# First image and its conv kernels ahead of the constants, constants on ScalarE's queue, attention weights in few transfers

## The chip, the cores and the metric

The kernel runs on one core of one Trainium2 chip. The metric is the device time of one launch in microseconds (us). The engines are TensorE (PE, with its weight loads PEld), VectorE (DVE), ScalarE (ACT), GpSimd (POOL) and SyncE (SP), which computes nothing and issues transfers (DMAs). Each engine takes its instructions in the order of its own queue; an instruction that waits holds everything behind it on that queue.

## The reference

There are 32 images of 128 channels by 64 x 64 pixels, in float32.

```
x = x + conv(group_norm(x))      # per-image 3x3 kernel: sum of 4 kernels with softmax(sigmoid(fc(mean))) weights
t = tokens(x)                    # 4096 tokens of 128 features an image
t = t + LN(z + gate * up(windowed_attention(down(z))))      # z = LN(t); window 144, stride 72, 4 heads of 4
t = t + scan(batch_norm(W LN(t)))                           # y = sigmoid(wx_t + V y), over the tokens of a row
```

The batch norm needs the statistics of all images, so the scan can't begin before the last image has gone through everything else.

## The kernel before, in words

**Constants and guards.** At the top, `ident` and masks made from it are computed, and 14 small tensors are fetched on SP's queue (`nc.sync.dma_start`; `column`, line 297, does the one-column ones). From some of these the kernel computes two flags on VectorE, ScalarE and TensorE (lines 353 to 403): `oki`, whether the attention scores are bounded so that no maximum has to be subtracted, and `okv`, whether the scan contracts so that it can be cut in runs. Each engine loads `oki` into a register and branches on it (line 1843) to `images`; `okv` is loaded before the second branch (line 1999), to `by_runs`.

**Images.** `images` (line 413) holds the first phase. Two frames of 66 x 66 pixels (`frames`, `xs`) take the images in turn. `fetch(b)` brings an image in 4 transfers of 16 rows; images 0 and 1 are fetched at the head of `images`, a later one at the head of its `load` (line 597). For each image there are 13 generators:

- `load`: group-norm statistics (`mv`, `gm`, `cv`), the routing weights `pl` and `co`, and the mixed conv kernel `h`, summed from four kernels of 576 KB, which `kernel()` (line 629) fetches into buffers called `place`. Two are asked for ahead of the statistics' second half and each further one when a buffer has been used.
- `taps` and `waves`: transformed kernels `w` and transformed inputs `u` of a short convolution that yields four output rows from six products. `conv`: the products on TensorE into the PSUM banks `nm`. `drain`: the results added into the frame.
- `project`: frame to DRAM (`x_d`), layer norm over channels, down-projection. `feed`, `values`, `attend`: queries and keys, values, and scores (`sc`), exponentials on ScalarE (`ex`, `ext`) and weighted sums (`av`). `divide0` and `divide1`: division and up-projection (`avs`).
- `tail` and `last`: the two layer norms behind the attention, the product with W (`fWc`), the results to DRAM (`z_d`, `out`).

**Setup.** `setup` (line 1267) is a job of its own. It builds what the attention needs: block-diagonal copies of the query, key and value weights (`wqB`, `wkB`, `wvB`: zero fill on GpSimd and 8 transfers of a 16 x 16 block each), repeated biases (`bqB`, `bkB`, `bd`: 8 transfers each), masks, the folded output weights `wc` (four products `wuT,aw` of TensorE, each followed by three steps of VectorE), and constants of `VT` (56 copies). `project` waits for it.

**The order of the work.** All jobs are Python generators that yield before each step what it needs: engine, PSUM pool, operands read and written. A planner at build time (lines 1385 to 1417) keeps a model of when each engine is free (class `Clock`) and always takes the step that it expects to be ready first; between equal ones it takes the smaller of "image number + due time", with the due times from the table `DUE` (line 41). So the queues are written out in full when the program is built, and a due time that is changed can move instructions anywhere. A job that isn't in the table, as `setup` isn't, comes ahead of all others that are ready at the same time. In the traces all planned instructions stand on line 241, the planner's wrapper.

**Second phase.** `by_runs` (line 1871) cuts the tokens in runs of 32 with 20 warming steps, and steps through them on TensorE, VectorE, ScalarE and GpSimd.

Of the kernel before, what the change touches and what calls it, by code (L numbers as in the profile page):

```python
# [20 lines left out]
NH = 4  # L21
HD = 4
DK = NH * HD
WIN = 144
HALF = WIN // 2
NWG = 7
# [4 lines left out]
NR = 20  # L31
NQ = 8
# [4 lines left out]
NI = 2  # L37
NSTR = 4


DUE = {
    "load": (-0.91, 0.63, 29),
    "taps": (-0.09, 0.03, 6),
    "waves": (-0.12, 0.52, 26),
    "conv": (-0.43, 1.01, 36),
    "drain": (-9.0, 0.0, 14),
    "project": (0.75, 0.5, 33),
    "feed": (1.63, 0.54, 27),
    "values": (1.27, 1.15, 28),
    "attend": (1.24, 1.1, 89),  # L50
    "divide0": (1.92, 0.12, 15),
    "divide1": (2.3, 0.02, 11),
    "tail": (2.55, 0.45, 33),
    "last": (3.05, 0.62, 40),
}

# [200 lines left out]
def hybrid_kernel(  # L257
# [24 lines left out]
    nc = tc.nc  # L282
# [7 lines left out]
    const = ctx.enter_context(tc.tile_pool(name="const", bufs=1))  # L290
# [5 lines left out]

    def column(src, name):
        t = const.tile([P, 1], F32, name=name)
        nc.sync.dma_start(t, src.rearrange("(c o) -> c o", o=1))
        return t  # L300


    ident = const.tile([P, P], F32, name="ident")
    make_identity(nc, ident)
# [15 lines left out]


    fcwT = const.tile([P, NK], F32, name="fcwT")
    nc.sync.dma_start(fcwT, fc_wT)
    fcb = const.tile([P, NK], F32, name="fcb")
    nc.sync.dma_start(fcb, fc_b.partition_broadcast(P))
    wd = const.tile([P, 32], F32, name="wd")
    nc.vector.memset(wd, 0.0)
    nc.sync.dma_start(wd[:, 0:DK], w_downT)
    gsig = const.tile([P, 1], F32, name="gsig")
    nc.sync.dma_start(gsig, gate.partition_broadcast(P))  # L330
# [8 lines left out]
    nc.sync.dma_start(fWT, ffn_WT)  # L339
    fVT = const.tile([P, P], F32, name="fVT")  # L340
    nc.sync.dma_start(fVT, ffn_VT)
    fg = column(ffn_gamma, "fg")
    fb = column(ffn_beta, "fb")

    bdr = const.tile([P, DK], F32, name="bdr")
    nc.sync.dma_start(bdr, b_down.partition_broadcast(P))
    ipr = const.tile([P, 3 * DK], F32, name="ipr")
    nc.sync.dma_start(ipr, in_proj_b.partition_broadcast(P))
    ipT = const.tile([DK, 3 * DK], F32, name="ipT")
    nc.sync.dma_start(ipT, in_projT)  # L350
# [36 lines left out]
    with tc.tile_pool(name="sb2", bufs=1) as sb2, tc.tile_pool(  # L387
        name="ps2", bufs=1, space=bass.MemoryType.PSUM
# [16 lines left out]
    small = nc.values_load(oki[0:1, 0:1], min_val=0, max_val=1)  # L405


    frames = const.tile([P, NI, (H + 2) * (W + 2)], F32, name="frames")
    framed = frames[:, :, 0:T]

    QT, NPL, NF, NZ, NU = T // 4, 5, 2, 3, 9

    def images(nc):
# [6 lines left out]
        with ExitStack() as pa:  # L420
# [3 lines left out]
            def rows(t, i, n=8):  # L424
                return t[:, 1 + i : 1 + i + n, 1 : W + 1]

            def fetch(b):
                for i in range(4):
                    nc.sync.dma_start(rows(xs[b % NF], 16 * i, 16), x[b, :, 16 * i : 16 * i + 16, :])

            fetch(0)


            for b in range(1, NF):
                fetch(b)
            keep = pa.enter_context(tc.tile_pool(name="keep", bufs=1))
            big = pa.enter_context(tc.tile_pool(name="big", bufs=NZ))
            one = pa.enter_context(tc.tile_pool(name="one", bufs=1))
# [7 lines left out]
            nc = clock  # L446
# [140 lines left out]
            def load(b):  # L587
# [5 lines left out]
                ):  # L593
                    yield
                gx = xs[b % NF]
                if b >= NF:
                    fetch(b)
                yield "DVE", None, (rows(gx, 0, H),)
                st = sml.tile([P, NBLK, 6], F32, name="st")
                for i in range(NBLK):  # L600
# [26 lines left out]
                taps = []  # L627

                def kernel():
                    w = yield from place("SP", ())  # L630
                    nc.sync.dma_start(w, conv_k[:, len(taps)].rearrange("m i j l -> m (i j l)"))
                    taps.append(w)

                for k in range(2):
                    yield from kernel()
                yield "PE", nms, (cv,)
                gv_ps = clock.take("PE", nms)
# [629 lines left out]
            def setup():  # L1267

                nonlocal wqB, wkB, wvB, bqB, bkB, bd, wd2, mqk, mvt, VEs, Vc, VTf, VT, wc, fWc, gbc, gbk, avg
                yield "SP", None, ()  # L1270

                wqkv = []
# [7 lines left out]
                bqB, bkB = kept([P, 1], "bqB"), kept([P, 1], "bkB")  # L1280
                bd = kept([P, 1], "bd", 0.0)
# [6 lines left out]
                in_b1 = in_proj_b.rearrange("(c o) -> c o", o=1)  # L1288
                for g in range(NQ):
                    r = slice(16 * g, 16 * g + 16)  # L1290
                    nc.sync.dma_start(bqB[r], in_b1[0:DK])
                    nc.sync.dma_start(bkB[r], in_b1[DK : 2 * DK])
                for g in range(NQ):
                    nc.sync.dma_start(
                        bd[16 * g : 16 * g + DK], b_down.rearrange("(c o) -> c o", o=1)
                    )

                mqk = kept([P, 2 * NH], "mqk")
                nc.vector.tensor_reduce(
                    mqk, memb.rearrange("p (q g) -> p g q", q=4), axis=AX.X, op=ALU.add  # L1300
                )

                m16 = kept([P, 8], "m16")
                nc.vector.tensor_reduce(
                    m16, ident.rearrange("p (g k) -> p g k", k=16), axis=AX.X, op=ALU.add
                )
# [11 lines left out]
                Vc = kept([P, NWG * NQ * DK], "Vc")  # L1318
                VTf = kept([P, NWG * NQ * NR + 32 - NR], "VT", 0.0)
                VT = VTf[:, 0 : NWG * NQ * NR].rearrange("p (w o) -> p w o", o=NR)  # L1320
                for q in range(4):
                    for u in range(2):
                        for m in range(NWG):
                            nc.vector.tensor_copy(
                                VT[:, NQ * m + 2 * q + u, DK:NR], mvt[:, NH * u : NH * (u + 1), 0]
                            )

# [19 lines left out]
                for q in range(4):  # L1347
                    r = slice(32 * q, 32 * q + DK)
# [36 lines left out]
            done, gone = {}, {}  # L1385
            pa.enter_context(tc.manual_schedule())
            jobs = [["setup", 0, setup(), None, 0]]
            for b in range(NB):
                for name, g in (
                    ("last", last(b)), ("tail", tail(b)), ("divide0", divide(b, 0)), ("divide1", divide(b, 1)), ("attend", attend(b)),  # L1390
                    ("project", project(b)), ("load", load(b)), ("conv", conv(b)), ("feed", feed(b)),
                    ("taps", taps(b)), ("waves", waves(b)), ("values", values(b)), ("drain", drain(b)),
                ):
                    jobs.append([name, b, g, None, 0])
            while jobs:
                near = min(j[1] for j in jobs) + 4
                best = None
                for job in jobs:
# [444 lines left out]
    with tc.If(small > 0) as arm:  # L1843
        images(nc)
# [212 lines left out]
```

## Time and profile before

| | us |
|---|---|
| median of 3 runs | 4645.3 |
| lowest and highest | 4629.8, 4645.8 |
| the profiled execution | 4639.8 |
| its span, first to last instruction | 4637.9 |
| TensorE busy | 4195.7 |
| VectorE busy | 3576.6 |
| ScalarE busy | 2503.6 |
| GpSimd busy | 1649.0 |
| first conv product of TensorE | 78.9 |
| last store of the first phase issued | 4040.2 |

The profile is of one execution. Its page gives the busy time of each engine, and the span in 40 slices of 116 us, with a digit for the tenths that are busy. The trace behind it can be asked for the busy time in any stretch, for the instructions in order of time (start, duration, engine, line, operation, output and inputs, and in brackets the idle time before it with what ended that), and for who waited for whom (total, times, longest). "SPq" is SP's issuing of a transfer, not the transfer itself. A time in a line that joins several instructions reaches from the first to the last.

### The profile page before, as it was taken

The page shows a single profiled execution, that of the slowest core. Times are in us where ns is not written, and L with a number is a line of the kernel's source. Part 1 is how long each engine was busy: PE and PEld are TensorE (multiplying, and loading weights), DVE is VectorE, ACT ScalarE, POOL GpSimd, SP SyncE. Part 2 cuts the span into 40 slices and gives each one's busy share as a digit, 9 for nine tenths or more (in the row PEclk, how much of TensorE's full clock was granted, in tenths as well). Part 3 has the DMA queues.
Part 4 walks back from the last instruction along what each step waited for, and adds up shares of the span by engine and source line. Part 5 has one row for each costly group of instructions (what it writes and reads, how often), then busy time and mean ns, then how long its engine had stood idle before and what let it go on. Part 6 is the DMA issues. An engine that isn't in the chain of part 4 may idle for free.

```text
span 4637.9 us, 102446 instructions
## 1 busy us (share of the span) xinstructions
PE 4195.7 (90%) x41527; PEld 2063.1 (44%) x41527; DVE 3576.6 (77%) x5472; ACT 2503.6 (54%) x4012; POOL 1649.0 (36%) x1656
## 2 busy tenths in 40 slices
PE   3999989999999999999999999999999997389995
PEld 1444444444444444444444444444444443145552
DVE  5877778888878877878887877878788854469994
ACT  0455555555555555545555455555555565258883
POOL 2433333333333333333333333333333321037674
PEclk9999999999999999999999999999999998679997
DMA  3434464554555555555555455555555453439997
GB/s 79 134 120 145 149 198 164 172 175 149 177 167 178 180 161 172 171 163 176 170 177 182 145 190 154 166 173 179 176 159 174 160 182 134 168 151 248 281 263 145
DMA packets 468568, 789.39 MB, mean 170 GB/s; under 512 B 339040, under 2 KB 349296, under 8 KB 435312
## 3 DMA queue, kind: packets, MB, share of 16 engines
q1 hardware_dynamic: 459376, 715.56, 47.3%
q0 software_dynamic: 8704, 67.11, 7.1%
q8 instruction: 332, 5.44, 0.5%
q14 instruction: 156, 1.28, 0.1%
HBM read 499.06 MB, written 276.76 MB: 167 GB/s over the span
## 4 chain that ended last, share of the span: by engine, by line
PE 26%; DVE 15%; DMA 7%; issue 3%; ACT 2%; SPq 2%; POOL 1%; DVEq 0%; ACTq 0%; POOLq 0%
PE nm L241 13%; PE sc L241 6%; PE av L241 4%; DVE v L1921 4%; DVE zt L241 3%; DVE v L1915 2%; SPq L241 2%; DMA place<-r_d 2%; PE v L1920 1%; DMA zr<-z_d 1%; DVE frames L241 1%; DMA place<-x_d 1%; DVE u L241 1%; ACT yw L1924 1%; DMA out_dram<-zr 1%
## 5 line engine op out<-in xcount | busy, mean ns | idle before, releaser
L241 ACT ACTIVATE ex<-sc 128x1152 f32<-128x1152 f32 x896 | 1013.6, 1131 | 879.9 <-PE sc L241 859.3
L241 POOL TENSOR_TENSOR qe<-qs,mqk 128x576 f32<-128x576 f32 x448 | 601.1, 1344 | 864.8 <-PE sc L241 856.3
L241 PE MATMUL nm<-u,w 128*128 128x512 f32 x1536 | 809.1, 631 | 18.9 <-POOL w L241 18.9
L241 PE MATMUL sc<-qe,ks 32*128 32x288 f32 x7168 | 698.0, 459 | 80.4 <-ACT ext L241 33.3
L241 PE MATMUL av<-ex,VE 128*32 128x144 f32 x14336 | 631.0, 294 | 29.7 <-DVE avs L241 29.1
L241 PEld LDWEIGHTS sc<-qe,ks 32*128 32x128 f32 x7168 | 284.9, 185 | 621.5 <-issue 168.0
L241 PEld LDWEIGHTS av<-ex,VE 128*32 128x32 f32 x14336 | 368.1, 110 | 369.1 <-issue 260.8
L241 POOL TENSOR_TENSOR u<-frames 128x528 f32<-128x528 f32 x256 | 374.4, 1475 | 154.8 <-PE nm L241 152.3
L241 PE MATMUL nm<-u,h 128*128 128x512 f32 x768 | 393.0, 620 | 0.0
L241 PEld LDWEIGHTS nm<-u,w 128*128 128x128 f32 x1536 | 253.2, 191 | 276.0 <-issue 245.1
L1920 PE MATMUL v<-yw,fVT 128*128 128x256 f32 x1024 | 327.6, 442 | 40.3 <-ACT yw L1924 39.1
L241 ACT ACTIVATE place<-zt 128x1024 f32<-128x1024 f32 x256 | 264.1, 1054 | 142.4 <-DVE zt L241 121.2
L241 DVE SCALAR_TENSOR_TENSOR u<-u,u 128x528 f32<-128x528 f32 x256 | 263.1, 1044 | 66.8 <-POOL u L241 65.2
L1925 POOL COPY zr<-yw 128x256 f32<-128x256 f32 x416 | 258.7, 689 | 123.4 <-ACT yw L1924 122.7
L1924 ACT ACTIVATE yw<-v,shf 128x256 f32<-128x256 f32 x512 | 242.3, 474 | 106.0 <-DVE v L1921 68.3
L241 PE MATMUL nm<-zt,fWc 128*128 128x512 f32 x512 | 286.5, 651 | 7.8 <-ACT zt L241 6.8
L1921 DVE SCALAR_TENSOR_TENSOR v<-zr,scl,v 128x256 f32<-128x256 f32 x416 | 257.3, 665 | 40.7 <-PE v L1920 40.0
L241 POOL TENSOR_TENSOR kt<-ks,mqk 128x384 f32<-128x384 f32 (+1 forms) x96 | 86.3, 899 | 492.5 <-ACT ks L241 439.4
L241 PE MATMUL nm<-place,avg 128*32 128x256 f32 x3072 | 246.8, 401 | 8.2 <-ACT place L241 7.9
L1914 PE MATMUL v<-yw,fVT 128*128 128x254 f32 x608 | 212.1, 449 | 46.1 <-ACT yw L1911 28.2
L241 DVE SCALAR_TENSOR_TENSOR zt<-sc,gbk,zt 128x576 f32<-128x576 f32 (+1 forms) x192 | 174.9, 911 | 98.0 <-PE sc L241 95.6
L1920 PEld LDWEIGHTS v<-yw,fVT 128*128 128x128 f32 x1024 | 159.8, 194 | 194.6 <-ACT yw L1924 188.3
(205 smaller groups left out, 6676.8 us busy)
## 6 DMA issues: line engine op xcount, KB each, us to landing
place<-r_d SPq DMA_DIRECT2D x384, 512.0 KB
place<-in_conv_k_dram SPq DMA_DIRECT2D x128, 576.0 KB
x_d<-frames SPq DMA_DIRECT2D x32, 2112.0 KB
place<-x_d SPq DMA_DIRECT2D x128, 528.0 KB
frames<-in_x_dram SPq DMA_DIRECT2D x128, 512.0 KB
out_dram<-zt SPq DMA_DIRECT2D x64, 1024.0 KB
z_d<-zt SPq DMA_DIRECT2D x64, 1024.0 KB
zr<-z_d SPq DMA_DIRECT2D x26, 2048.0 KB
```

Of the source, the lines that this page charges most:

```text
L241: got = f(*args, **kw)
L1914: nc.tensor.matmul(ps, fVT, yw[1 - r % 2][:, :, 1:], start=True, stop=True)
L1915: nc.vector.scalar_tensor_tensor(ps, z, scl, ps, ALU.mult, ALU.add)
L1920: nc.tensor.matmul(ps, fVT, yw[1 - r % 2], start=True, stop=True)
L1921: nc.vector.scalar_tensor_tensor(ps, zt[:, :, :, r], scl, ps, ALU.mult, ALU.add)
L1924: nc.scalar.activation(yw[r % 2], ps, AF.Sigmoid, bias=shf)
L1925: nc.gpsimd.tensor_copy(zt[:, :, :, r], yw[r % 2])
```

## The change

Five things are altered; the arithmetic of the images stays.

1. The frames are allocated at the top, and image 0 is fetched there on SP's queue before anything else. Image 1 is fetched at the head of its `load`, as later images are.
2. The 14 constants are fetched by ScalarE's queue.
3. Image 0 asks for its four conv kernels at once at the head of `load`. A fetch of a later image is a step of its own that the planner places.
4. `setup` fetches the in-projection weights with one transfer that repeats them over 8 groups of partitions (`rep`), and each repeated bias with one; the block-diagonal weights are products of `rep` with a mask on VectorE. The 56 copies into `VT` become two. `setup` gets an entry in `DUE`, and waits until image 0's taps are done before it makes the weights.
5. Due times of `taps`, `project`, `divide1` and `tail` are changed.

```diff
 DUE = {
+    "setup": (0.2, 0.2, 8),
-    "taps": (-0.09, 0.03, 6),
+    "taps": (0.2, 0.11, 6),
...
-    "project": (0.75, 0.5, 33),
+    "project": (0.55, 0.51, 33),
...
-    "divide1": (2.3, 0.02, 11),
-    "tail": (2.55, 0.45, 33),
+    "divide1": (2.21, 0.02, 11),
+    "tail": (2.4, 0.8, 33),
...
     def column(src, name):
         t = const.tile([P, 1], F32, name=name)
-        nc.sync.dma_start(t, src.rearrange("(c o) -> c o", o=1))
+        nc.scalar.dma_start(t, src.rearrange("(c o) -> c o", o=1))
...
+    frames = const.tile([P, NI, (H + 2) * (W + 2)], F32, name="frames")
+    framed = frames[:, :, 0:T]
+    for i in range(4):
+        nc.sync.dma_start(
+            frames[:, 0].rearrange("p (h w) -> p h w", w=W + 2)[:, 1 + 16 * i : 17 + 16 * i, 1 : W + 1],
+            x[0, :, 16 * i : 16 * i + 16, :],
+        )
...
-    nc.sync.dma_start(fcwT, fc_wT)
+    nc.scalar.dma_start(fcwT, fc_wT)
...
-            fetch(0)
-            for b in range(1, NF):
-                fetch(b)
...
                 gx = xs[b % NF]
-                if b >= NF:
+                if b:
+                    yield "SP", None, (), (rows(gx, 0, H),)
                     fetch(b)
+                taps = []
+                def kernel():
...
+                if b == 0:
+                    for k in range(NK):
+                        yield from kernel()
...
-                for k in range(2):
+                for k in range(2 if b else 0):
                     yield from kernel()
...
-                    if k + 2 < NK:
+                    if len(taps) < NK:
                         yield from kernel()
...
+                def eight(t, a):
+                    n, w = int(a.shape[0]), int(a.shape[1])
+                    nc.sync.dma_start(
+                        t, a.rearrange("(g d) w -> g d w", g=1).to_broadcast([NQ, n, w])
+                    )
...
+                rep = kept([P, 3 * DK], "rep")
+                eight(rep, in_projT)
+                bqB, bkB, bd = kept([P, 1], "bqB"), kept([P, 1], "bkB"), kept([P, 1], "bd")
+                in_b1 = in_proj_b.rearrange("(c o) -> c o", o=1)
+                eight(bqB, in_b1[0:DK])
+                eight(bkB, in_b1[DK : 2 * DK])
+                eight(bd, b_down.rearrange("(c o) -> c o", o=1))
+                while ("taps", 0, 1) not in done:
+                    yield
+                yield "DVE", None, (rep,)
                 wqkv = []
                 for i, n in enumerate(("wqB", "wkB", "wvB")):
-                    t = kept([P, P], n, 0.0)
-                    for g in range(NQ):
-                        r = slice(16 * g, 16 * g + 16)
-                        nc.sync.dma_start(t[r, r], in_projT[:, i * DK : (i + 1) * DK])
+                    t = kept([P, P], n)
+                    nc.vector.tensor_mul(
+                        t.rearrange("p (g k) -> p g k", k=DK),
+                        rep[:, i * DK : (i + 1) * DK].rearrange("p (g k) -> p g k", g=1).to_broadcast([P, NQ, DK]),
+                        m16.rearrange("p (g k) -> p g k", k=1).to_broadcast([P, NQ, DK]),
+                    )
                     wqkv.append(t)
...
-                for q in range(4):
-                    for u in range(2):
-                        for m in range(NWG):
-                            nc.vector.tensor_copy(
-                                VT[:, NQ * m + 2 * q + u, DK:NR], mvt[:, NH * u : NH * (u + 1), 0]
-                            )
+                yield "DVE", None, ()
+                for u in range(2):
+                    nc.vector.tensor_copy(
+                        VT.rearrange("p (w u) o -> p w u o", u=2)[:, :, u, DK:NR],
+                        mvt[:, NH * u : NH * (u + 1), 0].rearrange("p (w h) -> p w h", w=1).to_broadcast([P, NWG * 4, NH]),
+                    )
```

The other constants change their queue as `fcwT` does.

More of the change, by code (lines that the diff above doesn't have):

```diff
@@ L322, in hybrid_kernel @@
     fcwT = const.tile([P, NK], F32, name="fcwT")
-    nc.sync.dma_start(fcwT, fc_wT)
+    nc.scalar.dma_start(fcwT, fc_wT)
     fcb = const.tile([P, NK], F32, name="fcb")
-    nc.sync.dma_start(fcb, fc_b.partition_broadcast(P))
+    nc.scalar.dma_start(fcb, fc_b.partition_broadcast(P))
     wd = const.tile([P, 32], F32, name="wd")
     nc.vector.memset(wd, 0.0)
-    nc.sync.dma_start(wd[:, 0:DK], w_downT)
+    nc.scalar.dma_start(wd[:, 0:DK], w_downT)
     gsig = const.tile([P, 1], F32, name="gsig")
-    nc.sync.dma_start(gsig, gate.partition_broadcast(P))
+    nc.scalar.dma_start(gsig, gate.partition_broadcast(P))
     nc.scalar.activation(gsig, gsig, AF.Sigmoid)
@@ L338, in hybrid_kernel @@
     fWT = const.tile([P, P], F32, name="fWT")
-    nc.sync.dma_start(fWT, ffn_WT)
+    nc.scalar.dma_start(fWT, ffn_WT)
     fVT = const.tile([P, P], F32, name="fVT")
-    nc.sync.dma_start(fVT, ffn_VT)
+    nc.scalar.dma_start(fVT, ffn_VT)
     fg = column(ffn_gamma, "fg")
@@ L345, in hybrid_kernel @@
     bdr = const.tile([P, DK], F32, name="bdr")
-    nc.sync.dma_start(bdr, b_down.partition_broadcast(P))
+    nc.scalar.dma_start(bdr, b_down.partition_broadcast(P))
     ipr = const.tile([P, 3 * DK], F32, name="ipr")
-    nc.sync.dma_start(ipr, in_proj_b.partition_broadcast(P))
+    nc.scalar.dma_start(ipr, in_proj_b.partition_broadcast(P))
     ipT = const.tile([DK, 3 * DK], F32, name="ipT")
-    nc.sync.dma_start(ipT, in_projT)
+    nc.scalar.dma_start(ipT, in_projT)
     okf = const.tile([P, 1], F32, name="okf")
@@ L405, in hybrid_kernel @@
     small = nc.values_load(oki[0:1, 0:1], min_val=0, max_val=1)
-    frames = const.tile([P, NI, (H + 2) * (W + 2)], F32, name="frames")
-    framed = frames[:, :, 0:T]
     QT, NPL, NF, NZ, NU = T // 4, 5, 2, 3, 9
@@ L595, in load @@
                 gx = xs[b % NF]
-                if b >= NF:
+                if b:
+                    yield "SP", None, (), (rows(gx, 0, H),)
                     fetch(b)
+                taps = []
+                def kernel():
+                    w = yield from place("SP", ())
+                    nc.sync.dma_start(w, conv_k[:, len(taps)].rearrange("m i j l -> m (i j l)"))
+                    taps.append(w)
+                if b == 0:
+                    for k in range(NK):
+                        yield from kernel()
                 yield "DVE", None, (rows(gx, 0, H),)
@@ L626, in load @@
                 done["mean", b] = gm, gm6
[L627 to L632, printed above, removed]
-                for k in range(2):
+                for k in range(2 if b else 0):
                     yield from kernel()
@@ L1270, in setup @@
                 yield "SP", None, ()
+                def eight(t, a):
[3 more added lines that the diff above has]
+                    )
+                m16 = kept([P, 8], "m16")
+                nc.vector.tensor_reduce(
+                    m16, ident.rearrange("p (g k) -> p g k", k=16), axis=AX.X, op=ALU.add
+                )
[9 more added lines that the diff above has]
+                yield "DVE", None, (rep,)
                 wqkv = []
                 for i, n in enumerate(("wqB", "wkB", "wvB")):
-                    t = kept([P, P], n, 0.0)
-                    for g in range(NQ):
-                        r = slice(16 * g, 16 * g + 16)
-                        nc.sync.dma_start(t[r, r], in_projT[:, i * DK : (i + 1) * DK])
+                    t = kept([P, P], n)
[4 more added lines that the diff above has]
+                    )
                     wqkv.append(t)
                 wqB, wkB, wvB = wqkv
-                bqB, bkB = kept([P, 1], "bqB"), kept([P, 1], "bkB")
-                bd = kept([P, 1], "bd", 0.0)
                 wd2 = kept([P, 48], "wd2", 0.0)
@@ L1287, in setup @@
                 nms.append(wdp)
[L1288 to L1295, printed above, removed]
-                    )
                 mqk = kept([P, 2 * NH], "mqk")
@@ L1300, in setup @@
                     mqk, memb.rearrange("p (q g) -> p g q", q=4), axis=AX.X, op=ALU.add
[L1301 to L1305, printed above, removed]
                 )
@@ L1320, in setup @@
                 VT = VTf[:, 0 : NWG * NQ * NR].rearrange("p (w o) -> p w o", o=NR)
-                for q in range(4):
-                    for u in range(2):
-                        for m in range(NWG):
-                            nc.vector.tensor_copy(
-                                VT[:, NQ * m + 2 * q + u, DK:NR], mvt[:, NH * u : NH * (u + 1), 0]
-                            )
+                yield "DVE", None, ()
[3 more added lines that the diff above has]
+                        mvt[:, NH * u : NH * (u + 1), 0].rearrange("p (w h) -> p w h", w=1).to_broadcast([P, NWG * 4, NH]),
+                    )
                 aw = kept([DK, DK], "aw")
```

## The prediction

> **What bounds the kernel now.** I read the page first (shares, slices), then the busy time by stages, then the order of time and the waits of the first 140 us, and last what TensorE (PE) waits for in the steady part.
>
> ```profile
> span 4637.9 us, 102446 instructions
> PE 4195.7 (90%) x41527; PEld 2063.1 (44%) x41527; DVE 3576.6 (77%) x5472; ACT 2503.6 (54%) x4012; POOL 1649.0 (36%) x1656
> PE   3999989999999999999999999999999997389995
> ```
>
> TensorE is the bound wherever its digit is 9. The first slice (3) and the passage between the phases (7, 3, 8) are not TensorE-bound. The stages say it in microseconds:
>
> ```profile
> 0.00:80.00 80.00, 9.99 (x31) 6.25 (x32) 35.48 (x141) 6.05 (x13) 15.12 (x35) 1.00 0.46 114
> 80.00:140.00 60.00, 53.43 (x175) 23.34 (x174) 53.66 (x87) 9.83 (x17) 26.03 (x21) 0.97 0.09 37
> 800.00:1400.00 600.00, 573.61 (x6189) 278.74 (x6182) 483.25 (x704) 323.58 (x492) 202.59 (x168) 0.99 0.53 168
> ```
>
> The columns are length, then busy time of PE, PEld, DVE, ACT, POOL, then clock, DMA share and GB/s. In the first 80 us TensorE works 10. From 80 to 140 VectorE (53.7 of 60) is as full as TensorE. In the steady part TensorE is busy 573.6 of 600. Why the start is empty, in order of time:
>
> ```profile
> 13.32 17.15 SPq L429 DMA_DIRECT2D frames<-in_x_dram  x8
> 28.31 0.37 DVE L241 BATCH_NORM_AGGREGATE mv<-st 128x2 f32<-128x48 f32 x1
> 30.59 6.04 SPq L241 DMA_DIRECT2D wqB<-in_in_projT_dram  x8
> 33.45 0.29 DVE L241 TENSOR_SCALAR pl<-dev,gr 128x128 f32<-128x128 f32 x1
> 57.32 17.84 SPq L241 DMA_DIRECT2D place<-in_conv_k_dram  x8
> 58.72 0.58 PE L241 MATMUL nm<-wuT,aw 16*16 16x128 f32 x2 [27.84 <-DMA wuT<-in_w_upT_dram]
> 65.33 0.59 PE L241 MATMUL nm<-fcwT,pl 128*128 128x4 f32 x2
> 69.14 1.83 DVE L241 TENSOR_SCALAR h<-place,co 128x1152 f32<-128x1152 f32 x1
> 76.34 1.10 POOL L241 TENSOR_TENSOR w<-h 128x384 f32<-128x384 f32 x1 [4.20 <-DVE h L241]
> 78.91 8.32 PE L241 MATMUL nm<-u,w 128*128 128x512 f32 x12 [12.50 <-POOL w L241]
> ```
>
> SP's queue issues from 30.6 to 57.3 one small weight transfer after another (48 for the attention, 4 more) ahead of the conv kernels. TensorE and VectorE have setup work in their queues ahead of the routing of image 0, and it waits for those transfers: `pl` is ready at 33.7, but its product starts at 65.3. The waits of 0 to 260 us name it:
>
> ```profile
> PE nm L241 <- DMA wuT<-in_w_upT_dram: 27.8, 1, 27.8
> DVE bv L241 <- DMA bv<-in_in_proj_b_dram: 23.6, 1, 23.6
> ```
>
> In the steady part (800 to 3800 us) TensorE waits little, mostly on the attention:
>
> ```profile
> PE sc L241 <- ACT ext L241: 22.0, 24, 1.8
> PE sc L241 <- ACT ex L241: 10.7, 20, 0.7
> PE sc L241 <- POOL qe L241: 6.8, 9, 1.9
> ```
>
> **What the Trainium skill says.** (1) "DMA: Bandwidth & Descriptors", section "Issuing engines are not separate DMA queues": transfers of SP and ACT share the same DMA engines; a second issuer saves only issue time. The trace agrees that issue is what is scarce at the start: about 0.46 us for each small transfer. (2) The same page, "Anatomy of one DMA": about 2 us fixed for a transfer (given there for the GpSimd path). Here `wd`, issued at 1.66, is used at 4.04: 2.4 us. (3) "Perfetto Trace Analysis", section "What 'DMA-bound' means": a solid sequencer track is descriptor generation. SP from 30.6 to 57.3 is that. (4) "TensorE: Matmul & The Clock Gate", section "What's actually happening": half clock after an idle window. Here the first 12 conv products take 8.32 us and the next 12 take 5.31; both kernels pay this once.
>
> **The change part by part.** The order of the built program gives the new queues; durations are the trace's.
>
> *Constants on ScalarE's queue.* 14 transfers at SP's pitch of 0.47 us (ACT-issued ones aren't in the trace; from 0.43, their busy time, to twice that) are 6.6 us, with a table load of 1.28 and `gsig` 0.2 among them. The semaphore lanes are shared: `fWT` waits for the image's first quarter, which lands about 5.3 us after its issue (13.32 to 18.64 in the trace), so at 6.1 instead of 4.0. That puts the last, `ipT`, at 10.4 instead of 6.9, and its Abs, 3.2 us later, at 13.7 instead of 10.1. From there the guard's results follow as before: `oki` 2.24 us later (15.9), `okv` 4.09 us later (17.8), since VectorE runs both before its branch. SP now reads `okv` too before it branches, with conv kernels queued behind that: issue at about 19. **Loss 3.6 us** on this chain; 0 to 8 with the image's bytes between.
>
> *Image 0 first.* It has landed by about 15, so statistics start at about 19: 8 x 0.61 + 0.28 = 5.2, `mv` starts at 24.2 against 28.3. The 56 VT copies (4.09 us) that lay between are gone. `pl` comes 5.4 us later as before (28.31 to 33.74): 29.7.
>
> *Kernels ahead of weights, setup later.* Four kernel issues from 19, landed by about 32 (the first by 24; 2.36 MB at some 200 GB/s, an estimate from the page's GB/s row). Nothing blocks TensorE's queue now: product and coefficients 3.8 us (65.33 to 69.14), `h` from 33.6, done 7.4 later, first conv 2.6 after that: **43.6 instead of 78.9, gain 35.3**. Image 1, issued behind the kernels, lands at about 42; VectorE asks for it at 44.6, after `h` and four waves. That cover is thin: late by 3 us costs 3.
>
> *What is moved.* Setup's arithmetic, before in the shadow of the SP queue, lies now inside image 0's conv, where VectorE is full: three masks at 0.3, VT 0.5, `wc` 4 x 0.82, copies and small ones 2.1: 6.8 us. The four `wuT,aw` products alternate with VectorE (it waits 0.7 us for each, 2.8 in all), which stops both queues: +1.7 of these beyond cover. GpSimd's fills (VE 1.2, VT 1.04, `wd`, `wc`, `avg` 0.5) move in between its waves; it is busy 26 of 60 there, so 0, or 2.8 if a wave waits for all of them. **Cost 8.5**, from 0 (hidden in image 1's latencies) to 13. The few weight transfers, now 8 instead of 52, come behind image 1's kernels, some 15 us before use. Net of the start: **-26.8** (-35 to -14).
>
> *Due times and the fetch as a planned step* change the order of all 32 images. I counted in the two orders. TensorE's changes of tile shape: 3276 before, 3227 after; a pair of conv products between attention groups takes 1.05 us against 0.87 in a row, so 0.09 a change: -4. Attention steps of images 2 to 29 with no other TensorE work beside them: 28 before, 49 after. The three waits above sum to 39.5 us over 24 images with 25 such steps, at most 1.6 a step; I take a quarter of that, since the work moved away fills other gaps (137 of 3000 us are idle): 21 x 0.4 = +8, from 0 to +33. Net **+4** (-25, if a sixth of that idle is recovered, to +33).
>
> *The end.* SP no longer loads `okv` between the phases, but VectorE's own load there (4041.9 to 4045.5) remains: 0. By-runs is unchanged.
>
> Sum: the profiled execution took 4639.8 (span 4637.9 and 1.9 around it): 4639.8 - 26.8 + 4 = **4617.0**. The runs' median is 4645.3, 5.5 above it, their lowest 4629.8; I leave the sum as it is.
>
> **The rivals.**
> - *The order eats the gain.* 21 more bare attention steps at the full 1.6 = +33, -4: 4642. For: the count. Against: only 39.5 us of such waits exist.
> - *The start gains half.* The constants' small packets share engines with 2 MB of image, and the branch comes 10 us later: 4627. For: the guard chain is now the longest. Against: `ipT` is issued when half the image has landed.
> - *Slower: the fetch goes behind other SP work.* It was emitted as soon as a frame was free; now it is a step that other transfers may pass. From the x_d store of an image to the fetch into its frame stand 44 transfers on average before and 45 after, but 55 or more in 8 images instead of 3: 5 x 25 x 0.5 us = 62 us of late statistics: 4639.8 - 26.8 + 62 = 4675. It decides from 1.7 us of TensorE idle an image (50 us over 30). For: such a wait holds VectorE's whole queue. Against: in VectorE's order nine instructions stand between freeing and use, seven before.
> - *Better than forecast.* Setup hidden and the order fills gaps: -35.3 - 20: 4584.
>
> **How the numbers follow.** Forecast 0.45 (4603 to 4631), order eats 0.18, half start 0.12, slower 0.12, better 0.13. A measurement here can tell about 0.5% from no change: 4622.1 and 4668.5. Faster: 0.35 of the forecast, 0.13, and 0.04 of the half start: 0.52. Same: 0.10 + 0.18 + 0.08 = 0.36. Slower 0.12. Range 4588 to 4652: it leaves out the slower case and half of the better one.
>
> **What would show it.** Right: first conv product at 41 to 47 us, SP issuing conv kernels at about 19, no wait on `wuT` over 3 us, image 0's frame finished at about 92 (119.2 before), phase two starting 20 to 30 us earlier. Wrong: `okv` after 22; VectorE waiting on image 1; TensorE busy under 570 in 600 us of the steady part; the statistics' wait for image transfers (24.3 us in 800 to 3800) doubled.

## The result, and the profile after

The changed kernel takes 4611.1 us (median of 9 runs, 4604.8 to 4625.1), the kernel before 4645.5 (9 runs, 4629.8 to 4657.7). The ratio is 0.9929 (95% interval 0.9913 to 0.9944): 0.7% faster. The profiled execution took 4604.8 us with a span of 4602.9; before it was 4639.8 and 4637.9.

The page's first slice of TensorE is now 5 instead of 3, and the rest looks alike:

```profile
span 4602.9 us, 102351 instructions
PE 4175.5 (91%) x41527; PEld 2065.4 (45%) x41527; DVE 3577.4 (78%) x5421; ACT 2492.7 (54%) x4012; POOL 1650.6 (36%) x1652
...
PE   5999999899899999999999999999999987379995
```

The busy time by stages, in the same columns as before:

```profile
0.00:80.00 80.00, 36.40 (x87) 16.84 (x87) 57.61 (x123) 8.05 (x16) 29.49 (x42) 0.97 0.45 114
80.00:140.00 60.00, 53.43 (x225) 23.21 (x226) 49.17 (x83) 11.72 (x22) 11.16 (x10) 0.89 0.36 108
800.00:1400.00 600.00, 562.38 (x6069) 274.63 (x6072) 485.19 (x703) 318.90 (x485) 205.28 (x167) 0.98 0.51 165
```

TensorE gains 26.4 us of work in the first 80 us. In the steady stretch shown it is less busy than before (562.4 against 573.6). The start in order of time (lines picked; start, length, engine, line and operation, and in brackets the idle time before it and what ended it):

```profile
5.81 0.34 ACTq L348 DMA_DIRECT2D fWT<-in_ffn_WT_dram  x1
13.17 0.24 ACT L377 ACTIVATE ipT<-ipT 16x48 f32<-16x48 f32 x1
17.11 0.15 DVE L410 CAST okv<-vm 128x1 int32<-128x1 f32 x1
18.14 1.86 SPq L242 DMA_DIRECT2D place<-in_conv_k_dram  x4
22.98 0.37 DVE L242 BATCH_NORM_AGGREGATE mv<-st 128x2 f32<-128x48 f32 x1
28.18 0.28 DVE L242 TENSOR_SCALAR pl<-dev,gr 128x128 f32<-128x128 f32 x1
28.52 0.59 PE L242 MATMUL nm<-fcwT,pl 128*128 128x4 f32 x2 [2.91 <-DVE pl L242]
32.03 1.82 DVE L242 TENSOR_SCALAR h<-place,co 128x1152 f32<-128x1152 f32 x1
41.78 7.12 PE L242 MATMUL nm<-u,w 128*128 128x512 f32 x12 [12.68 <-POOL w L242]
53.28 0.35 PE L242 MATMUL nm<-mv,grp 128*128 128x1 f32 x2 [1.80 <-DVE mv L242]
54.33 4.38 PE L242 MATMUL nm<-u,h 128*128 128x512 f32 x6 [0.69 <-DVE frames L242]
75.91 0.39 PE L242 MATMUL nm<-wuT,aw 16*16 16x128 f32 x2 [1.05 <-DVE wc L242]
95.50 3.20 PE L242 MATMUL nm<-frames,avg 128*32 128x256 f32 x26 [5.45 <-DVE frames L242]
```

Nothing stands between `pl` and its product any more (28.5 against 65.3), and the first conv product comes at 41.8 instead of 78.9. The last line marks that image 0's frame is finished: 95.5 against 119.3. The same mark in the kernel before:

```profile
119.27 3.19 PE L241 MATMUL nm<-frames,avg 128*32 128x256 f32 x26 [5.07 <-DVE frames L241]
```

Three marks cut every profile below into parts: that last line, the last `z_d` store, the end. The **middle** (between the first two) holds the same 39,784 TensorE products in every kernel here.

| us | start | middle | phase two |
|---|---|---|---|
| before | 119.3 | 3920.9 | 597.7 |
| changed | 95.5 | 3915.1 | 592.3 |
| difference | -23.8 | -5.8 | -5.4 |

Phase two has the same 1632 products in all 14 profiles of this study and takes 590.0 to 604.5, so its -5.4 is not put down to the change. Nor is the -5.8, as the repeats below show. What the change gives for certain is the start, some 24 us. It need not be all: the medians, taken side by side three times (here and with e3 and e8), differ by 34, 41 and 29 us. That is 5 to 17 us more than the start, and single profiles don't show where it comes from.

### The profile page after: what moved, and what is told of

Same layout as the page of the kernel before. It is cut to its first block, busy times and chain, and to the rows that moved or that the text cites. A ratio compares the mean times of both kernels' runs of the same rounds, so it can differ in the third digit from the quotient of the medians.

```text
span 4602.9 us, 102351 instructions
## 1 busy us (share of the span) xinstructions
PE 4175.5 (91%) x41527; PEld 2065.4 (45%) x41527; DVE 3577.4 (78%) x5421; ACT 2492.7 (54%) x4012; POOL 1650.6 (36%) x1652
## 4 chain that ended last, share of the span: by engine, by line
PE 60%; DVE 20%; DMA 9%; ACT 4%; issue 4%; POOL 2%; SPq 1%; ACTq 0%; DVEq 0%; POOLq 0%
PE nm L242 35%; PE sc L242 14%; PE av L242 10%; DVE zt L242 4%; DVE v L1933 4%; DMA place<-r_d 3%; DVE v L1927 2%; ACT ex L242 2%; DVE frames L242 2%; DMA out_dram<-zr 2%; DVE u L242 1%; PE v L1932 1%; SPq L242 1%; DMA zr<-z_d 1%; DVE cp L242 1%
## 5 line engine op out<-in xcount | busy, mean ns | idle before, releaser
L242 DVE SCALAR_TENSOR_TENSOR u<-u,u 128x528 f32<-128x528 f32 x256 | 244.3, 967 | 46.4 <-POOL u L242 44.9
L242 ACT COPY zt<-nm 128x512 f32<-128x512 f32 x256 | 149.5, 585 | 206.7 <-PE nm L242 204.0
```

Of the source, the lines that this page charges most:

```text
L242: got = f(*args, **kw)
```

## The experiments

The changed kernel was run again beside the first experiments (e3); e8 turned out to be another repeat.

| | start | middle | TensorE idle in it | median, us | ratio to before (95%) |
|---|---|---|---|---|---|
| before | 119.3 | 3920.9 | 266 | 4645 to 4652 | 1 |
| changed | 95.5 | 3915.1 | 273 | 4611.1 | 0.9913 to 0.9944 |
| e3 changed again | 94.3 | 3924.4 | 276 | 4611.6 | 0.9895 to 0.9924 |
| e8 changed again | 95.9 | 3934.2 | 275 | 4618.3 | 0.9915 to 0.9946 |
| e1 old due times | 96.1 | 3982.8 | 313 | 4670.6 | 1.0026 to 1.0057 |
| e2 before, new due times | 121.5 | 3981.8 | 313 | 4702.7 | 1.0101 to 1.0131 |
| e4 setup in shadow | 86.8 | 3964.0 | 315 | 4651.4 | 0.9988 to 1.0006 |
| e5 the same, order held | 94.6 | 3922.7 | 272 | 4617.9 | 0.9920 to 0.9950 |
| e6 constants on SP | 100.5 | 3919.8 | 275 | 4623.4 | 0.9931 to 0.9964 |
| e7 guard first | 92.9 | 3926.5 | 268 | 4611.3 | 0.9905 to 0.9943 |
| e9 shadow, picked order | 88.6 | 3894.8 | 261 | 4582.9 | 0.9836 to 0.9881 |
| e10 before, picked order | 119.2 | 3836.6 | 217 | 4552.5 | 0.9772 to 0.9815 |
| e11 attend due time | 94.6 | 3984.4 | 315 | 4671.8 | 1.0029 to 1.0065 |
| e12 last due time | 94.2 | 3937.9 | 287 | 4621.3 | 0.9920 to 0.9955 |

### Start and order apart: e1, e2, e3

e1 is the changed kernel with the old due times; e2 is the kernel before with the new ones (the same lines the other way round).

```diff
-    "taps": (0.2, 0.11, 6),
+    "taps": (-0.09, 0.03, 6),
...
-    "project": (0.55, 0.51, 33),
+    "project": (0.75, 0.5, 33),
...
-    "divide1": (2.21, 0.02, 11),
-    "tail": (2.4, 0.8, 33),
+    "divide1": (2.3, 0.02, 11),
+    "tail": (2.55, 0.45, 33),
```

> The changed kernel with the four old due times (taps, project, divide1, tail); the start stays changed. My theory: the gain is made in the first 100 us and the order of the other images is worth only a few us either way. Then the first conv product stands at 41.8 us and frame 0 is finished at 95 us, as in the changed kernel, and the total is 4604 to 4628 (ratio to the kernel before 0.991 to 0.996). Rival: the start is worth little at the end because the planner gives it back, and it is the new order that brings the gain: 4632 to 4646, not told from the kernel before.

> The kernel before with the four new due times alone; the start is that of before. My theory: first conv product at 78.9 us, frame 0 finished at 119 us, total within 10 us of the kernel before (4635 to 4655, ratio 0.998 to 1.002). Rival (the order is the gain): 4610 to 4625, ratio 0.993 to 0.996.

> The changed kernel itself, beside the others on the same chip. Both theories: ratio 0.991 to 0.995. Its second profile tells what repeats: I expect first conv product and frame 0 within 0.5 us of 41.8 and 95.4, and the times of the last images to differ by up to 10 us from the first profile.

e3 repeated as expected (ratio 0.991, first conv product at 41.7). Of e1 and e2 both theories fell. The starts came nearly as expected (first conv product at 42.7 and 78.9), but e1 took 4670.6 and e2 4702.7: each part alone makes the kernel slower (ratios 1.004 and 1.012), and together they make it 0.7% faster. So the new start with the old due times loses more than it gained: some 60 us in the middle.

```profile
96.11:4078.88 3982.77, 3669.37 (x39784) 1788.36 (x39784) 3033.46 (x4409) 2089.41 (x3157) 1278.77 (x1066) 0.96 0.51 163
```

This is e1's middle. In the changed kernel the same products take:

```profile
95.50:4010.58 3915.08, 3642.15 (x39784) 1789.18 (x39784) 3031.04 (x4405) 2086.79 (x3157) 1284.74 (x1065) 0.97 0.51 166
```

TensorE is idle for 313 us instead of 273 and busy 27 us longer on the same work. A new theory was needed: an order of the 32 images is worth up to 60 us, and each of the two kernels compared carries one that goes with its start. That is a reading of these two runs; the later ones test it.

### The setup inside image 0's conv: e4 and e5

e4 does the chain of four products and their VectorE sums (`wc`, `gbc`, `gbk`) ahead of the branch, and fetches for it at the top; the guard's constants go first on ScalarE's queue:

```diff
+    aw_ = sb0.tile([DK, DK], F32, name="aw")
+    nc.sync.dma_start(aw_, out_proj_w)
...
+        for q in range(4):
+            r = slice(32 * q, 32 * q + DK)
+            nc.tensor.matmul(wps[r], aw_, wuT_, start=True, stop=True)
...
-                yield "PE", nms, (aw, wuT)
-                wps = clock.take("PE", nms)
...
+                wc, gbc, gbk = wc_, gbc_, gbk_
```

> The changed kernel with the guard's constants first on ScalarE's queue, the setup's weights fetched at the top on both queues, and the four small products with their VectorE steps (wc, gbc, gbk) done ahead of the branch; the masks stay where they are. My theory: what the setup costs inside image 0's conv is 13 us, of which about 8 are the chain that goes to and fro between TensorE and VectorE; so frame 0 is finished at 86 to 90 us instead of 95.4, with the first conv product at 40 to 44, and the total is 4 to 9 us under the changed kernel's. Rival: the added transfers and VectorE steps come ahead of the guard's chain and of the statistics, so that the first conv product comes at 46 or later, frame 0 at 95 or later, and nothing is gained.

The start was as expected (first conv product 44.1, frame 0 at 86.8), the total was not: 4651.4, because the steps taken out changed the order of everything after them, and the middle took 3964. e5 makes the same edit but leaves the planner's bookkeeping of the removed steps in place:

```diff
+                def ghost(eng, op):
+                    return lambda *args, **kw: clock.note(eng, op, args, kw)
...
-                    nc.tensor.matmul(wps[r, 0:P], aw, wuT, start=True, stop=True)
+                    ghost("PE", "matmul")(wps[r, 0:P], aw, wuT, start=True, stop=True)
```

> The same edit as in the run with the setup in the guard's shadow, but the planner is told the removed steps as if they were still there, so that the order of all images on every queue is word for word that of the changed kernel. My theory: with the order held, the start's gain passes through to the end: first conv product at 44, frame 0 finished at 86 to 88 us (changed kernel 95.4), total 7 to 9 us under the changed kernel's, about 4603 (ratio to the kernel before 0.988 to 0.990). Rival: an earlier frame 0 is lost again before the last image, because the order has no use for it: total as the changed kernel's, or, if it was the setup's new place and not the order that cost 40 us in the other run, 4640 and more.

The middle is back at 3922.7, so the 40 us were the order's. But frame 0 came at 94.6, not at 86 to 88, and the total is that of the changed kernel. The stretch from the first conv product to the finished frame, in the kernel before, the changed kernel, e5 and e4 (columns as above):

```profile
78.91:119.27 40.36, 35.29 (x82) 15.41 (x82) 34.57 (x63) 3.38 (x9) 16.42 (x13) 1.00 0.01 2
41.78:95.50 53.72, 42.12 (x98) 18.55 (x99) 45.67 (x99) 3.37 (x9) 19.59 (x28) 0.88 0.05 19
43.89:94.55 50.66, 39.06 (x86) 16.48 (x87) 44.20 (x80) 3.48 (x9) 20.44 (x27) 0.91 0.00 1
44.12:86.84 42.72, 37.05 (x87) 15.88 (x87) 39.05 (x73) 3.48 (x9) 18.71 (x27) 0.93 0.00 0
```

With the chain in place and the same order the stretch took 51.8 to 53.7 us in five profiles (the changed kernel, e3, e6 to e8), so taking the chain out in a held order is worth 1 to 3 us. The other 8, between e5 and e4, lie in how the changed kernel's order lays image 1's steps among image 0's: the edit of the two is the same. In the changed kernel VectorE does image 1's statistics first while the conv waits (1.80 and 0.69 us at 53.3); in e4 the product of these statistics comes at 69.8, without a wait. Later in e5 TensorE waits 3.1 us for `pl`. On VectorE in e5:

```profile
80.42 1.26 DVE L242 TENSOR_TENSOR gl<-gr 128x1 f32<-128x1 f32 x1
81.71 1.32 DVE L242 SCALAR_TENSOR_TENSOR gl<-gv,gl 128x1 f32<-128x1 f32 x1
83.07 0.15 DVE L242 TENSOR_SCALAR gl<-gl 128x1 f32<-128x1 f32 x1
```

and on GpSimd in e5:

```profile
77.35 4.31 POOL L242 TENSOR_TENSOR u<-frames 128x528 f32<-128x528 f32 x3
81.61 0.15 POOL L242 MEMSET avg<- 128x64 f32 x1
81.71 1.31 POOL L242 TENSOR_TENSOR u<-frames 128x528 f32<-128x528 f32 x1
```

The two one-column operations, 0.16 us each in the changed kernel, end when GpSimd's operation ends. Up to the copy ahead of them (`gv`) e5 is 5.6 us ahead of the changed kernel, counted from the first conv product; 2.3 of these are lost in the two operations.

### Parts of the start with the order held: e6, e7, e8

e6 puts the constants back on SP's queue; e7 moves the guard's five ahead of the others; e8 was meant to change the order a little. Of e6 one of the 14 constants is shown.

```diff
...
-    nc.scalar.dma_start(ipT, in_projT)
+    nc.sync.dma_start(ipT, in_projT)
```

> The changed kernel with its 14 constants back on SP's queue, behind image 0; the order of all later work is the same. My theory: the last constant is issued at about 15.5 us instead of 9.3, the guard's results and the statistics come some 5 us later, first conv product at 46 to 48 us instead of 41.8, frame 0 at 99 to 101, and the total 4 to 6 us over the changed kernel's. Rival: the guard chain has slack behind the image, and the first conv product and the total stay as in the changed kernel.

```diff
...
+    nc.scalar.dma_start(ipT, in_projT)
+    fVT = const.tile([P, P], F32, name="fVT")
+    nc.scalar.dma_start(fVT, ffn_VT)
     fcwT = const.tile([P, NK], F32, name="fcwT")
     nc.scalar.dma_start(fcwT, fc_wT)
```

> The changed kernel with the five constants of the guard first on ScalarE's queue; the order of all later work is the same. My theory: the last of them is issued at about 2.7 us, the guard's second result comes 1 to 4 us earlier than 17.1 (then the image's own landing, about 14 us, is next), first conv product at 38 to 41, total 1 to 4 us under the changed kernel's. Rival: the guard's arithmetic then waits for table loads or for the other constants that VectorE takes first, and nothing moves.

```diff
-    "feed": (1.63, 0.54, 27),
+    "feed": (1.63, 0.53, 27),
```

> The changed kernel with one due time changed in its last digit (feed 0.54 to 0.53): nothing that could matter by its size. My theory: each order of the 32 images is a draw with a spread of some 20 us and more, and the two kernels compared each carry one that fits; the start is then as in the changed kernel (first conv product 41.8, frame 0 95.4), and the total 10 to 60 us over it, 4620 to 4670. Rival: what counts is the size of the due times, and a change in the last digit leaves the total within 5 us of the changed kernel.

**e8** is no test of an order: a due time only decides between steps that the planner's clock puts at the same moment, and this one decided nothing; TensorE's order is the same to the last product. It serves as a repeat. Six profiles with this order (the changed kernel, e3, e5 to e8) have middles of 3915 to 3934 us, so 10 us either way is what one profile can't tell. Most of this spread is TensorE's clock: the changed kernel and e8, with the same queues throughout, are idle for 273 and 275 us in the middle, but busy for 3642 and 3660. The traces' clock records grant TensorE half its clock for 215 and 255 us of it, 153 and 193 of these busy. At half clock the conv products start every 0.86 us instead of 0.43, so half of the 40 us, 20, is an estimate of what this costs; the busy time differs by 17.5.

**e6**: `ipT` issued at 16.5, first conv product at 48.3, frame 0 at 100.5, about as expected. The total is 5.1 us over e8 beside it, but the intervals overlap; what the queue is worth is shown at the start (5 us), not at the end.

**e7**: `ipT` was issued at 2.16 instead of 9.26, but ScalarE then waited for `gsig`'s transfer with a table load at 8.52 and a second one at 11.01, so `okv` came at 16.5 (17.1) and the first conv product at 41.2. The rival was right in the main: the repeats have `okv` at 17.0 and 17.5, and the constants' place moves it by about 1 us at most.

### Orders: e9 to e12

e9 takes e4's idea again (its small weights by ScalarE's queue) with due times that fit; e10 is the kernel before with due times found in the same way, and nothing else:

```diff
-    "load": (-0.91, 0.63, 29),
+    "load": (-0.91, 0.83, 29),
...
-    "waves": (-0.12, 0.52, 26),
+    "waves": (-0.12, 0.72, 26),
...
-    "project": (0.75, 0.5, 33),
+    "project": (0.75, 0.7, 33),
...
-    "values": (1.27, 1.15, 28),
+    "values": (1.17, 1.25, 28),
...
-    "tail": (2.55, 0.45, 33),
+    "tail": (2.55, 0.67, 33),
```

> The setup's products and sums in the guard's shadow once more (its small weights by ScalarE's queue behind the guard's constants, so that image 0 is not held up; masks and their weights as in the changed kernel), now with due times that fit this start: of some 900 sets the one for which the kernel's own planner clock ends the plan first. My theory: a changed start needs an order made for it, and then its gain is kept: first conv product at 41 to 44, frame 0 at 84 to 88 us, the part from there to the last z_d store at 3915 us or less, total 4570 to 4605. Rival: the planner's clock can't tell a good order from a bad one on the chip, any order that wasn't picked on the chip costs 40 to 60 us: total 4640 to 4660.

> The kernel before with due times picked in the same way (nothing else changed). My theory: the order is worth as much as the start; first conv product stays at 78.9 us, the part from frame 0 to the last z_d store gets shorter than 3921 us, total 4600 to 4640. Rival: as with the four new due times on this start, some 50 us slower: 4690 to 4710.

e9 took 4582.9 with a middle of 3894.8, as my theory had it, though its first conv product came at 46.2 and frame 0 at 88.6, both late: VectorE did the setup's sums before the guard's and `okv` came at 21.6. e10 surprised: 4552.5, 2.1% under the kernel before without any change of the start (first conv product at 79.5), and below the range expected. Its middle:

```profile
119.17:3955.73 3836.56, 3619.91 (x39784) 1771.01 (x39784) 3050.81 (x4418) 2086.77 (x3159) 1325.26 (x1065) 0.98 0.53 169
```

Both kernels whose order was picked by the planner's clock beat both kernels compared, and of the five orders that nobody picked (e1, e2, e4, e11, e12) none comes near them. Two picks don't show how far that clock can be trusted.

e11 and e12 are the changed kernel with one due time moved by 0.02 so that the order does change:

```diff
-    "attend": (1.24, 1.1, 89),
+    "attend": (1.24, 1.08, 89),
```

```diff
-    "last": (3.05, 0.62, 40),
+    "last": (3.03, 0.62, 40),
```

> The changed kernel with one due time moved by 0.02 (attend 1.10 to 1.08), which here does change the order, from the second image's attention on. By the counts that the prediction used (37 bare attention steps against 49, 3219 tile-shape changes against 3227) it should be some 5 us faster than the changed kernel: 4603 to 4612. My theory now: those counts don't measure an order, and one that nobody picked costs 30 to 60 us: 4640 to 4675. First conv product and frame 0 stay at 41.8 and 95.4 in both.

> The changed kernel with another due time moved by 0.02 (last 3.05 to 3.03), which changes the order later on. By the prediction's counts (57 bare steps against 49, 3179 tile-shape changes against 3227): within 4 us of the changed kernel. My theory: an order that nobody picked, 20 to 60 us slower: 4630 to 4670, and the waits that grow are those of TensorE on zt, on GpSimd's w and on the last attention, as in the two other slow orders.

e11 took 4671.8, 60 us more than the changed kernel, with the same start (first conv product 42.9, frame 0 94.6). By the prediction's counts it should have been 5 us faster. e12 took 4621.3 with a middle of 3937.9: at most a little slower, under what I expected. Of the waits I named, TensorE's on `zt` before scores did not grow (39.9 us, in the changed kernel 39.5), the one on `w` did by 4. So not every change of order is dear.

Where an order's price lies is seen in TensorE's groups over the middle, the scores first: busy time and mean, then the idle time before them. The order of e10:

```profile
L241 PE MATMUL sc<-qe,ks 32*128 32x288 f32 x7168 | 694.7, 457 | 52.5 <-ACT ex L241 23.9 <-ACT ext L241 17.0 <-DVE zt L241 7.2
L241 PE MATMUL nm<-place,avg 128*32 128x256 f32 x3072 | 234.0, 387 | 4.2 <-ACT place L241 4.1
```

and of e11:

```profile
L242 PE MATMUL sc<-qe,ks 32*128 32x288 f32 x7168 | 707.1, 464 | 119.1 <-ACT ext L242 34.5 <-ACT ex L242 29.9 <-DVE zt L242 24.4
L242 PE MATMUL nm<-place,avg 128*32 128x256 f32 x3072 | 242.2, 394 | 20.2 <-ACT place L242 19.9
```

Between these two, TensorE's idle time differs by 98.5 us (216.7 and 315.2), 66.6 of it ahead of the scores; the busy time for the same products differs by 49.3. In a tighter order the attention's exponentials, its masked queries (`qe`) and the sums into `zt`, which read PSUM banks of the scores' pool, are done when their turn comes.

## Why the prediction was right, and where it was not

It forecast 4617.0 and the change gave 4611.1, inside the range. Two terms of the sum did not hold, and one of these was judged by a method that the runs refute. Luck helped the number: the sum was taken from the profiled execution (4639.8), 5.7 us under the median of the kernel before. The change itself was forecast at -22.8 and measured at -34.4 between medians, -35.0 between profiles; of these 12 us the start has +3.0, the middle -9.8 and phase two -5.4.

- **Constants on ScalarE's queue, image 0 first, kernels ahead of weights** (first conv product at 43.6): right, and right by its steps. `ipT` was issued at 9.3 (10.4) and took longer to its Abs, 3.9 us (3.2); so its Abs stands at 13.2 (predicted 13.7), `okv` 17.1 (17.8), SP's kernels 18.1 (19), `mv` 23.0 (24.2), `pl` 28.2 (29.7), `h` from 32.0 (33.6), product 41.8. `fWT` waited for the image's first quarter as forecast (5.8 against 6.1). The gain is 37.1 instead of 35.3. No run takes back the kernels' or the setup's place alone, so that these make most of it is read from the order of time; the constants' queue alone was tried, and is worth 5 us at frame 0 (e6).
- **Image 1 behind the kernels, cover thin**: right; VectorE takes it at 45.4 without a wait on its transfer.
- **What is moved, 8.5 (0 to 13)**: mis-sized. From the first conv product to the finished frame the changed kernel takes 53.7 us against 40.4: 13.4. TensorE is busy 6.8 us longer in it and idle 6.5 longer. Of the 6.8, 3.4 are setup's own 16 products and 3.4 the same 72 conv products. The chain itself is worth 1 to 3 (e5); what the prediction missed is the order of image 1's steps in that stretch (8 us between e5 and e4), and that TensorE pays for half its clock more than once: six conv products take 4.38 us after the waits at 53.3, and 2.74 elsewhere, and the clock records have half clock from 55.5 to 58.9 and from 79.4 to 86.2, where the kernel before has none between 84.8, its first record, and 118.9. The prediction had it that both kernels pay this once.
- **Net of the start, -26.8**: -23.8 measured.
- **Due times and the fetch, +4 (-25 to +33)**: this step failed as a method, though its range held. The middle measured -5.8, with repeats 19 us apart, so +4 itself is not refuted. But its counts do not rank the orders:

| | bare attention steps | tile-shape changes | middle, us |
|---|---|---|---|
| e10 | 28 | 3268 | 3837 |
| e9 | 38 | 3207 | 3895 |
| before | 28 | 3276 | 3921 |
| changed | 49 | 3227 | 3915 to 3934 |
| e12 | 57 | 3179 | 3938 |
| e4 | 78 | 3207 | 3964 |
| e2 | 55 | 3226 | 3982 |
| e1 | 46 | 3264 | 3983 |
| e11 | 37 | 3219 | 3984 |

The waits that they stood for did grow, and by more than the 8 us counted. In 800 to 3800 us of the changed kernel:

```profile
PE sc L242 <- ACT ext L242: 28.2, 28, 1.4
PE sc L242 <- ACT ex L242: 23.7, 41, 3.0
PE av L242 <- DVE avs L242: 18.1, 11, 5.3
PE sc L242 <- POOL qe L242: 14.0, 14, 3.5
PE nm L242 <- DVE pl L242: 8.2, 4, 2.7
```

The three attention waits went from 39.5 to 65.9 us, and that of the scores on `zt` from 15.1 to 25.4; others fell, `avs` from 26.4 to 18.1, `pl` from 16.9 to 8.2. Over the whole middle TensorE's idle time rose by 7 us only (266 to 273). A sum over one kind of wait is not what an order costs. The sign "TensorE busy under 570 in 600 us" came up in two of five stretches (562.4 and 564.3), and the middle was no longer for it; the kernel before has one such stretch too (567.2).
- **The range's ends, -25 and +33, were too near**: with one due time moved the same start gives a middle 60 us longer (e11), and on the old start another order is worth -84 (e10).
- **The rivals.** Slow fetch: out; VectorE's wait for image transfers in 800 to 3800 us is 20.4 us (24.3 before). Half start: out; `okv` comes 3.1 us later than before (17.1 and 14.0), not the branch 10. "The order eats the gain" was the right worry: e1 is that case, at 4670.6 beyond what the rival allowed (4642). "Better than forecast" (4584) did not come with this change; e9 reached it with another order.

So that the change came out faster rests on something the prediction took for small: that the due times shipped with the change give an order as good as the old one was for the old start. What makes an order good stays open here: the profile says where TensorE waits in a bad one, but neither count ranked these nine.

The Trainium skill, "TensorE: Matmul & The Clock Gate", section "What's actually happening", has the clock at half after an idle window. The middles agree: the mean granted clock is 0.96 or 0.97 where TensorE is idle for 313 to 315 us (e1, e2, e4, e11) and 0.98 where it is 217 (e10), and 98.5 us less idle come with 49.3 us less busy time. The clock records account for the second number: TensorE is busy at half clock for 94 us in e10's middle and for 208 in e11's, and half of the difference, 57 us by this estimate, is somewhat more than the 49.3. Between these two orders the one that waits more pays half as much again in clock; no run changes the clock alone.

## What to carry to other kernels

Where a planner writes the order of the work, an edit at one place can be two: its own effect, to be read at the place (here -24 us), and a new order for everything behind it, worth 60 us one way and 84 the other in these runs; hold the order fixed to measure the first, and pick a new order before judging the second. Before working on a start or on one wait, see what another order of the old kernel gives: here that alone (2.1%) was worth nearly three times the change. A repeat of the same program tells what a single profile can't tell apart.

## What the runs showed of the hardware that was not expected

- A one-column VectorE operation on two tensors (`gl`, 0.16 us) took 1.26 and 1.32 us in e5 while GpSimd ran an operation on frames, and ended with it; a copy from PSUM with one input took 0.15 in the same GpSimd stretch (`gv`, at 77.7). The Trainium skill, "GPSIMD Engine Reference", section "1. Specifications", has GpSimd's way to the buffers shared with VectorE operations that have two such inputs; the trace agrees, at a price of 1.1 us for an operation of 0.16.
- TensorE's clock was halved at 55.5 us although it had worked for 1.5 of the 3.4 us before (the waits of 1.80 and 0.69 us lie there), so the idle window named above need not be idle throughout. It is no fixed price either: e8 has the same at 55.8, e3, the same program, has none before 74.9.
- Small transfers cost ScalarE's queue what they cost SP's in the kernel before: 0.44 to 0.45 us each (0.43), at a pitch of about 0.48 (0.47).
- Two queues can hold each other. The four image transfers at the top took SP 9.1 us to issue (8.6 and 9.5 in e8 and e7), 7.3 of which it waited for constants on ScalarE's queue to land:

```profile
SPq L307 <- DMA fcwT<-in_fc_wT_dram: 3.0, 1, 3.0
SPq L307 <- DMA fWT<-in_ffn_WT_dram: 2.7, 1, 2.7
SPq L307 <- DMA gsig<-in_gate_dram: 1.6, 1, 1.6
```

In the trace the first transfers of both queues go through the same eight semaphores in turn, so the image waits for constants as `fWT` waits for the image. The prediction had only the second. In e6, where ScalarE's queue had nothing to issue, SP waits for none of them, but each of the last three image transfers takes 2.2 to 2.7 us to issue, 7.7 for the four.
